# An LSTM step on TensorE: the first half's product for the second bank is cut into column pieces, and the last piece goes behind the second half's product for the first bank

## Chip, cores and metric

One Trainium2 chip, one of its cores. The metric is the time of one execution on the device in microseconds (us), as the median of several runs.

## The reference, cut to what matters

The kernel runs two graph layers, a state-space layer and at last an LSTM: `x` is (32, 512, 256), so the LSTM has a batch of 32, 512 time steps and 256 hidden units. Only the last layer is touched:

```python
def _lstm(x, W_ih, W_hh, b_ih, b_hh):
    x_proj = jnp.einsum('btd,gd->btg', x, W_ih) + b_ih + b_hh
    h0 = jnp.zeros((x.shape[0], W_hh.shape[1]), x.dtype)
    c0 = jnp.zeros_like(h0)
    def step(carry, xp):
        h, c = carry
        gates = xp + h @ W_hh.T
        i, f, g, o = jnp.split(gates, 4, axis=-1)
        c = jax.nn.sigmoid(f) * c + jax.nn.sigmoid(i) * jnp.tanh(g)
        h = jax.nn.sigmoid(o) * jnp.tanh(c)
        return ((h, c), h)
    _, hs = jax.lax.scan(step, (h0, c0), jnp.swapaxes(x_proj, 0, 1))
    return jnp.swapaxes(hs, 0, 1)
lstm_out = _lstm(x, W_ih, W_hh, b_ih, b_hh)
logits = jnp.einsum('bth,lh->btl', lstm_out, W_lin) + b_lin
g = argmax(logits, axis=-1)[..., None]
w = g * lstm_out
inc = jnp.cumsum(w, axis=1)
prefix, suffix = inc - w, inc[:, -1:, :] - inc
return 2.0 * lstm_out + prefix * fw_att + suffix * bw_att
```

The result is added to the layer's input `x`; the LSTM reads a layer-normalised `x`.

## The kernel before

The layers ahead of the LSTM run batch by batch and leave their result in a DRAM tensor `X3`, and the LSTM's weights, laid out anew, in `wr`. The function `recurrence` then goes through the 512 time steps, one after another, with the order of instructions on TensorE, VectorE and ScalarE written out by hand (`manual_schedule`). Each engine works through its own instructions in the order in which the code gives them.

**Layout of a step.** 256 hidden units are four quarters q of J = 64 units. The state of quarter q and the 32 batches lies on partitions 32q to 32q + 31, so gates and cell state fill all 128 partitions. Each quarter has two halves of H = 32 units. Of the gates of a quarter, 3H = 96 columns are g, f and i of the first half; the next 96 are g, f and i of the second half; then come 64 columns of o, for both halves, and two columns of which the first gives the difference of the two logits: W = 258 columns in all. They lie in two PSUM tiles, given by

```python
PARTS = ((0, 3 * H), (3 * H, W))
```

Bank 0 (`pg0`) has the 96 columns of the first half's g, f, i. Bank 1 (`pg1`) has 162 columns: g, f, i of the second half (0:96 within the bank), o of the first half (96:128), o of the second half (128:160) and the logit's two (160:162).

**Matmuls.** `h` is a list of two tiles, h0 and h1: the transposed state of the first and of the second halves, 128 x 32 each, the stationary operands. `part` (L1238) takes a list `order` of pairs (k, n): half k's product for bank n. For each pair it issues four matmuls, one for each quarter q, with 32 stationary columns each, into the 32 partitions of that quarter. In the trace each of these matmuls is two records of MATMUL and two of LDWEIGHTS. `x_part` (L1248) does the same for the input's part of the next time step. A step's state part has the order (0,0), (0,1), (1,0), (1,1) (L1295): both banks from h0, then both banks from h1.

**A step in order.**
- TensorE: the state part of this step (needs h0, and from (1,0) on h1), the input part of the next step, and in 4 of 16 steps two transposes of a coming input (L1181).
- ScalarE: tanh of bank 0 (L1302) into the tile `z`; tanh of 160 columns of bank 1 (L1303); tanh of the new cell state of each half (L1313, twice); a copy of one column (L1315).
- VectorE: for each half `ab` (L1308) and the new cell state in `z` (L1311). Then for each half `hh`, the new state (L1321), and its 32 x 32 transpose into `h` (L1325): first half 0, then half 1. After that `g` (L1332), one piece of other work out of the list `extra`, and `pp` (L1338), the running sum.

`extra` holds 16 pieces, one for each of 16 steps: 4 of `stats` (L1166 and L1167), 2 of `both` (two of L1172 each), and 10 of `results` for the 16 steps before (L1208 to L1220). In the first of the 16 steps a copy (L1340) comes on top.

The sigmoids are written with tanh, with factors of 0.5 in the weights, so all gates take one function.

Of the kernel before, what the change touches and what calls it, by code (L numbers as in the profile page):

```python
# [33 lines left out]
GB = 32  # L34
# [1085 lines left out]
def recurrence(ctx, tc, c, a, X3, wr, out):  # L1120
# [6 lines left out]
    H = J // 2  # L1127
    W = 4 * J + 2
# [13 lines left out]
    wih, whh = (wall[:, n * nw : (n + 1) * nw].rearrange("p (k q w) -> p k q w", k=DK, q=Q) for n in range(2))  # L1142
# [10 lines left out]
    def normalised(t0, out_):  # L1153


        mv = small.tile([P, NX, 2], F32, tag="mv", name=f"mv{t0}")
        rs = [None]
        xs = []
        for n in range(NX):
            xt = xp_.tile([P, D], F32, tag=f"xt{n}", bufs=1, name=f"xt{t0}_{n}")  # L1160
            nc.sync.dma_start(out=xt, in_=X3[t0 + 4 * n : t0 + 4 * n + 4].rearrange("t b d -> (t b) d"))
            xs.append(xt)

        def stats(n):
            bs = small.tile([P, 6], F32, tag="bs", name=f"bs{t0}_{n}")
            nc.vector.bn_stats(bs, xs[n])  # L1166
            nc.vector.bn_aggr(mv[:, n, :], bs)  # L1167
            if n == NX - 1:
                rs[0] = rstd_of(nc, small, c, mv[:, :, 1], NX, LN_EPS)

        def norm(n):
            nc.vector.tensor_scalar(  # L1172
                xs[n], xs[n], mv[:, n, 0:1], rs[0][:, n : n + 1], ALU.subtract, ALU.mult
            )
            nc.gpsimd.memset(xs[n][:, D - 1 :], 1.0)

        def turn(n):

            pt = psx.tile([P, DK, P], F32, tag="px", name=f"pxt{t0}_{n}")
            for k in range(DK):  # L1180
                nc.tensor.transpose(pt[:, k, :], xs[n][:, k * P : (k + 1) * P], c.ident)  # L1181
            g, r = n // 2, n % 2 * P
            if not r:
                out_[g] = xp_.tile([P, DK, 2 * P], F32, tag=f"xT{g}", name=f"xTr{t0}_{g}")
            xT = out_[g][:, :, r : r + P]
            return lambda: nc.scalar.copy(xT, pt)

        return tuple([lambda f=f, n=n: f(n) for n in range(NX)] for f in (stats, norm, turn))
# [48 lines left out]

    def part(pg, w, lhs, order, start, stop):  # L1238

        for k, n in order:  # L1240
            p, (s, e) = pg[n], PARTS[n]
            for q in range(Q):
                nc.tensor.matmul(  # L1243
                    p[q * GB : (q + 1) * GB, :], lhs[k], w[:, k, q, s:e],
                    start=(start and k == 0), stop=(stop and k == DK - 1),
                )

    def x_part(t, xT):  # L1248

        pg = [psg.tile([P, e - s], F32, tag=f"pg{n}", name=f"pg{n}_{t}") for n, (s, e) in enumerate(PARTS)]  # L1250
        r = (t % G) * GB
        part(pg, wih, [xT[t % CH // G][:, k, r : r + GB] for k in range(DK)], ((0, 0), (1, 0), (0, 1), (1, 1)), True, t == 0)
        return pg

    with tc.manual_schedule(engines={mybir.EngineType.PE, mybir.EngineType.DVE, mybir.EngineType.Activation}):
# [9 lines left out]
        pg = x_part(0, nxt)  # L1265
# [7 lines left out]
        h = hh = None  # L1273
        for t in range(T + 1):
            s = t % CH
            last = t == T
            if s == 0 and not last:
                t0 = t
                hh_was, pp_was = hh, pp
                hh = ch.tile([P, CH, J], F32, tag="hh", name=f"hh{t0}")  # L1280
                if t:
                    pp = ch.tile([P, CH + 1, J], F32, tag="pp", name=f"pp{t0}")
                assert not extra and not turning
                xT, nxt = nxt, [None] * 2
                stats, norms, turns = normalised(t0 + CH, nxt) if t0 + CH < T else ([], [], [])
                more = results(t0 - CH, hh_was, pp_was) if t else []
                both = [lambda fs=norms[n : n + 2]: [f() for f in fs] for n in range(0, len(norms), 2)]
                extra = stats + both + more
                turning = {(5, 6, 10, 11)[n]: f for n, f in enumerate(turns)}
            if last:  # L1290

                pg = [None, psg.tile([P, W - 3 * H], F32, tag="pg1", name="pglast")]
                part(pg, whh, h, ((0, 1), (1, 1)), True, True)
            elif t:
                part(pg, whh, h, ((0, 0), (0, 1), (1, 0), (1, 1)), False, True)  # L1295
            pgs = pg
            if not last:
                if t + 1 < T:
                    pg = x_part(t + 1, xT if t + 1 < t0 + CH else nxt)
                turned = [turning.pop(s)()] if s in turning else []  # L1300

                nc.scalar.activation(z[:, H : 4 * H], pgs[0], AF.Tanh)  # L1302
                nc.scalar.activation(z[:, 5 * H : 10 * H], pgs[1][:, : 5 * H], AF.Tanh)  # L1303
                z2 = st.tile([P, 12 * H + 1], F32, tag="z", name=f"z{t + 1}")
                for n in range(2):
                    c0 = 4 * n * H
                    ab = st.tile([P, 2 * H], F32, tag=f"ab{n}", name=f"ab{n}_{t}")
                    nc.vector.scalar_tensor_tensor(  # L1308
                        ab, z[:, c0 + 2 * H : c0 + 4 * H], 1.0, z[:, c0 : c0 + 2 * H], ALU.add, ALU.mult
                    )  # L1310
                    nc.vector.scalar_tensor_tensor(z2[:, c0 : c0 + H], ab[:, :H], 0.5, ab[:, H:], ALU.mult, ALU.add)  # L1311
                for n in range(2):
                    nc.scalar.activation(z[:, (10 + n) * H : (11 + n) * H], z2[:, 4 * n * H : (4 * n + 1) * H], AF.Tanh, scale=0.5)  # L1313

                nc.scalar.copy(z2[:, 12 * H :], level)  # L1315
                for f in turned:
                    f()
                h = []
                for n in range(2):
                    half = hh[:, s, n * H : (n + 1) * H]  # L1320
                    nc.vector.scalar_tensor_tensor(  # L1321
                        half, z[:, (8 + n) * H : (9 + n) * H], 1.0, z[:, (10 + n) * H : (11 + n) * H], ALU.add, ALU.mult
                    )
                    h.append(st.tile([P, GB], F32, tag=f"h{n}", name=f"h{n}_{t}"))
                    nc.vector.transpose(h[n], half)  # L1325
                z = z2
            if t:

                i = (t - 1) % CH
                p_, h_ = (pp_was, hh_was) if s == 0 and not last else (pp, hh)  # L1330
                g_ = st.tile([P, J], F32, tag="g", name=f"g{t}")
                nc.vector.scalar_tensor_tensor(  # L1332
                    g_, pgs[1][:, 5 * H : 5 * H + 1].to_broadcast([P, J]), level, h_[:, i, :], ALU.is_gt, ALU.mult,
                )
            if extra and not last:
                extra.pop(0)()
            if t:
                nc.vector.tensor_tensor(p_[:, i + 1, :], p_[:, i, :], g_, ALU.add)  # L1338
                if s == 0 and not last:
                    nc.vector.tensor_copy(pp[:, 0, :], p_[:, CH, :])  # L1340
# [5 lines left out]
        for n in range(4 * Q):  # L1346
            tq, q = n // Q, n % Q
# [20 lines left out]
@with_exitstack  # L1368
def kernel(ctx: ExitStack, tc: tile.TileContext, a, out):
    nc = tc.nc  # L1370
    nb = a.x.shape[0]
    const = ctx.enter_context(tc.tile_pool(name="const", bufs=1))
    dram = ctx.enter_context(tc.tile_pool(name="dram", bufs=1, space=DRAM))
    c = setup_consts(nc, const)
    X3 = dram.tile([N, nb, D], F32, name="X3")
    wr = dram.tile([P, 2 * DK * 4 * 258 + 2 * 64 + 1], F32, name="wr")
    odd = const.tile([1, 1], I32, name="odd")
    with ExitStack() as phase:
        layers_per_batch(phase, tc, c, a, X3, odd, wr)
    general = nc.values_load(odd, min_val=0, max_val=1, skip_runtime_bounds_check_because="it is only compared with 0")  # L1380
    with tc.If(general > 0):
        with ExitStack() as phase:
            layers_per_batch(phase, tc, c, a, X3)
    with ExitStack() as phase:
        recurrence(phase, tc, c, a, X3, wr, out)
# [70 lines left out]
```

## Time and profile before

| | us |
|---|---|
| median of 3 runs | 4697.27 (4695.42 to 4697.93) |
| profiled execution | 4702.24 |
| its span, first to last instruction | 4700.4 |

| engine | busy us over the span | share |
|---|---|---|
| PE (TensorE, matmul) | 3892.5 | 83% |
| PEld (TensorE, weight loads) | 2418.6 | 51% |
| DVE (VectorE) | 3388.8 | 72% |
| ACT (ScalarE) | 2926.4 | 62% |
| POOL (GpSimd) | 1332.6 | 28% |

| rows of the recurrence | records | mean ns |
|---|---|---|
| L1243 MATMUL, from h, 96 columns | 8176 | 252 |
| L1243 MATMUL, from h, 162 columns | 8176 | 301 |
| L1302 tanh of bank 0 | 512 | 251 |
| L1303 tanh of bank 1 | 512 | 305 |
| L1308 `ab` | 1024 | 221 |

A row of the profile's groups names the line of the kernel, the engine and the operation, what is written and read, the shapes and the count; behind the first bar stand the time in which at least one of them ran and the mean duration of one in ns, behind the second the idle time of the engine just before them, with what ended it. [...] The order in time shows runs of like instructions as one line: start in us from the span's start, length, engine, line.

### The profile page before, as it was taken

What the parts mean: (1) busy time and instruction counts of PE and PEld (TensorE: products, weight loads), DVE (VectorE), ACT (ScalarE), POOL (GpSimd) and SP (SyncE); (2) the same over time, 40 slices, a digit from 0 to 9 for tenths busy, and PEclk for the clock granted to TensorE, in tenths of its full rate; (3) what the DMA queues carried; (4) which work ended last, traced back from release to release, by engine and by line L of the source; (5) the groups of instructions that cost most, each with busy time, mean ns of one, the idle gap of its engine ahead of it and who ended that gap; (6) DMA issues with size and microseconds to landing.
All of it is one profiled execution on the core that took longest, in us unless ns stands there. A gap on an engine that the chain in (4) does not pass through costs nothing. (4 is left out here: it accounts for less than half of the span.)

```text
span 4700.4 us, 115757 instructions
## 1 busy us (share of the span) xinstructions
PE 3892.5 (83%) x46798; PEld 2418.6 (51%) x46798; DVE 3388.8 (72%) x10205; ACT 2926.4 (62%) x6724; POOL 1332.6 (28%) x1148
## 2 busy tenths in 40 slices
PE   3788888888888888888888888888688888888883
PEld 2344444444444544444444444444466666666662
DVE  3466676666666666666666676666489999999997
ACT  2577777777777777776677776766444444444442
POOL 3433333433333433333433333432100000000000
PEclk7899999999999999999999999999799999999997
DMA  4222111222111222111122211211212222222225
GB/s 114 60 64 71 59 59 57 64 73 71 59 59 57 64 73 71 59 59 57 58 70 70 64 62 57 63 51 50 63 35 44 44 44 46 46 47 44 44 42 164
DMA packets 273754, 288.69 MB, mean 61 GB/s; under 512 B 151872, under 2 KB 224536, under 8 KB 271032
## 3 DMA queue, kind: packets, MB, share of 16 engines
q1 hardware_dynamic: 269832, 271.32, 20.3%
q10 hardware_dynamic: 3216, 9.81, 0.7%
q8 instruction: 372, 6.09, 0.5%
q14 instruction: 174, 1.43, 0.1%
q0 software_dynamic: 160, 0.04, 0.0%
HBM read 227.09 MB, written 37.11 MB: 56 GB/s over the span
## 5 line engine op out<-in xcount | busy, mean ns | idle before, releaser
L1243 PE MATMUL pg<-wall,h 128*32 128x96 f32 x16352 | 559.2, 277 | 176.7 <-DVE h L1325 169.3
L1243 PEld LDWEIGHTS pg<-wall,h 128*32 128x32 f32 x16352 | 374.8, 109 | 350.3 <-DVE h L1325 331.8
L1243 PE MATMUL pg<-wall,xTr 128*32 128x96 f32 (+1 forms) x16384 | 549.0, 274 | 0.0
L467 DVE SCALAR_TENSOR_TENSOR w<-w,adjT 128x1024 f32<-128x1024 f32 x256 | 348.1, 1380 | 247.6 <-ACT w L461 247.6
L1243 PEld LDWEIGHTS pg<-wall,xTr 128*32 128x32 f32 x16384 | 447.7, 110 | 4.9 <-issue 0.3
L743 ACT ACTIVATE g<-bc,cs 128x128 f32<-128x128 f32 x1024 | 321.9, 391 | 137.3 <-PE py L811 137.3
L1302 ACT ACTIVATE z<-pg 128x96 f32<-128x96 f32 x512 | 128.7, 251 | 439.3 <-PE pg L1243 439.3
L693 DVE SCALAR_TENSOR_TENSOR acc<-px,convw,acc 128x511 f32<-128x511 f32 (+2 forms) x480 | 347.2, 745 | 75.8 <-ACT acc L688 68.0
L461 ACT ACTIVATE w<-rb,neg,colsa 128x512 f32<-128x512 f32 x512 | 387.4, 806 | 9.9 <-DMA rb<-linea 6.0
L729 POOL TENSOR_TENSOR ce<-ce,cT 128x384 f32<-128x384 f32 x128 | 185.2, 1477 | 667.7 <-ACT cT L701 650.5
L533 PE MATMUL pav<-w,hb 128*64 128x512 f32 x1024 | 352.5, 615 | 22.5 <-DVE w L467 22.5
L830 PE MATMUL po<-wc,xh 128*128 128x256 f32 x1024 | 283.4, 422 | 100.2 <-POOL xh L800 100.2
L1313 ACT ACTIVATE z<-z 128x32 f32<-128x32 f32 x1024 | 234.7, 229 | 168.0 <-DVE z L1311 100.8
L945 PE MATMUL pov<-wb,wv 128*128 128x257 f32 x1024 | 243.1, 390 | 89.3 <-DVE wv L467 89.3
L54 POOL TENSOR_SCALAR ve<-mv 128x4 f32<-128x4 f32 x32 | 6.2, 195 | 1064.1 <-DVE mv L1167 1064.1
L672 PE MATMUL px<-mT,win 128*128 128x512 f32 x640 | 305.2, 607 | 0.0
L830 PEld LDWEIGHTS po<-wc,xh 128*128 128x128 f32 x1024 | 203.2, 213 | 145.3 <-POOL xh L800 115.6
L945 PEld LDWEIGHTS pov<-wb,wv 128*128 128x128 f32 x1024 | 191.5, 192 | 133.1 <-DVE wv L467 105.3
L56 POOL TENSOR_TENSOR rs<-ve,mhalf 128x4 f32<-128x4 f32 (+1 forms) x192 | 255.2, 1329 | 15.9
L800 POOL TENSOR_TENSOR xh<-xh,zs 128x512 f32<-128x512 f32 x128 | 175.5, 1381 | 282.1 <-DVE xh L799 282.1
L1325 DVE STREAM_TRANSPOSE h<-hh 128x32 f32<-128x32 f32 x1024 | 216.7, 212 | 34.9
L672 PE MATMUL pz<-mT,win 128*128 128x512 f32 x512 | 240.4, 602 | 0.0
(243 smaller groups left out, 8492.0 us busy)
## 6 DMA issues: line engine op xcount, KB each, us to landing
bc<-line SPq DMA_DIRECT2D x128, 512.0 KB
adj<-in_adj_dram SPq DMA_DIRECT2D x32, 1024.0 KB
rb<-linea SPq DMA_DIRECT2D x64, 512.0 KB
ce<-line SPq DMA_DIRECT2D x64, 384.0 KB
x<-in_x_dram SPq DMA_DIRECT2D x32, 512.0 KB
X<-x SPq DMA_DIRECT2D x32, 512.0 KB
xt<-X SPq DMA_DIRECT2D x128, 128.0 KB
x<-X SPq DMA_DIRECT2D x128, 128.0 KB
```

The costliest lines, as they stand in the source:

```text
L56: nc.gpsimd.tensor_tensor(rs, ve, c.mhalf[:, :n], ALU.pow)
L461: nc.scalar.activation(w[:, t, k, :], rb[:, k, :], AF.Relu, bias=neg1, scale=cols[:, 2 * m + t, h + k : h + k + 1],)
L467: nc.vector.scalar_tensor_tensor(w[:, :, k, :], w[:, :, k, :], 1.0, edges, ALU.add, ALU.mult)
L533: nc.tensor.matmul(pa[k * HO : (k + 1) * HO, :], hb[:, j, 2 * q + k, :], w[:, t, k, :], start=(j == 0), stop=(j == NT - 1),)
L672: nc.tensor.matmul(pz, win[:, k, col : col + P], mT[:, k, :], start=(k == 0), stop=(k == DK - 1))
L693: nc.vector.scalar_tensor_tensor(acc[:, s:], pz[:, : N - s], convw[:, cc, k : k + 1], acc[:, s:], ALU.mult, ALU.add)
L743: nc.scalar.activation(g[:, i, k, :], bc[:, k, i * P : (i + 1) * P], AF.Relu, bias=cs[:, i, 2 * cc + k : 2 * cc + k + 1], scale=-1.0,)
L830: nc.tensor.matmul(po[:, i * D : (i + 1) * D], xh[:, cc, it * P : (it + 1) * P], wc[:, cc, :], start=(cc == 0), stop=(cc == NC - 1),)
L945: nc.tensor.matmul(po[:, : D + 1], ws[j // 2][:, j % 2, 0, it * P : (it + 1) * P], wb[:, j, :], start=(j == 0), stop=(j == NT - 1),)
L1243: nc.tensor.matmul(p[q * GB : (q + 1) * GB, :], lhs[k], w[:, k, q, s:e], start=(start and k == 0), stop=(stop and k == DK - 1),)
L1313: nc.scalar.activation(z[:, (10 + n) * H : (11 + n) * H], z2[:, 4 * n * H : (4 * n + 1) * H], AF.Tanh, scale=0.5)
L1325: nc.vector.transpose(h[n], half)
```

## The change

`part` takes entries with two more numbers, the first and the last column within the bank, and without them uses all columns as before. In the state part of every step from the second on, half 0's product for bank 1 comes in column pieces: 0:96 and 96:128 follow (0,0), then comes (1,0), and 128:162, the second half's o and the logit's columns, comes behind it, ahead of (1,1). Each piece is four matmuls, one for each q, with weight loads of their own. The input part and the last step give pairs.

```diff
     def part(pg, w, lhs, order, start, stop):
 
-        for k, n in order:
+
+        for k, n, *columns in order:
             p, (s, e) = pg[n], PARTS[n]
+            c0, c1 = columns or (0, e - s)
             for q in range(Q):
                 nc.tensor.matmul(
-                    p[q * GB : (q + 1) * GB, :], lhs[k], w[:, k, q, s:e],
+                    p[q * GB : (q + 1) * GB, c0:c1], lhs[k], w[:, k, q, s + c0 : s + c1],
                     start=(start and k == 0), stop=(stop and k == DK - 1),
                 )
...
             elif t:
-                part(pg, whh, h, ((0, 0), (0, 1), (1, 0), (1, 1)), False, True)
+                of_o = 3 * H, 4 * H, W - 3 * H
+                order = (0, 0), (0, 1, 0, of_o[0]), (0, 1, *of_o[:2]), (1, 0), (0, 1, *of_o[1:]), (1, 1)
+                part(pg, whh, h, order, False, True)
```

## The prediction

> **What bounds the kernel now.** I read the page for where the end is set, then the groups of the last stage with shapes kept apart, then one step of that stage in order of time, then the starts of single matmuls in the trace. All times below are from the profiled execution, 4702.24 us (span 4700.4, 1.84 us around it); the median of the runs is 4697.27, 5 us less. I take a saving per step from the profile and subtract it from the median.
>
> The change touches only the recurrence: 512 steps, from about 3410 us to 4640 us. The window 3850 to 4250 us lies inside it:
>
> ```profile
> core 0: us, PE busy (x) PEld busy (x) DVE busy (x) ACT busy (x) POOL busy (x), PEclk, DMA share, GB/s
> ...
> 3850.00:4250.00 400.00, 343.12 (x10716) 274.80 (x10708) 374.70 (x1897) 197.59 (x873) 18.81 (x60) 1.00 0.21 44
> ```
>
> DVE is busy 374.7 of 400 us, PE has its full clock (1.00). So VectorE is nearly full while the step is also a loop of dependences through TensorE and ScalarE. Which of the two ends last is read from the groups:
>
> ```profile
> L1243 PE MATMUL pg<-wall,h 128*32 128x162 f32 x7632 | 431.0, 301 | 0.0
> L1243 PE MATMUL pg<-wall,h 128*32 128x96 f32 x7632 | 345.6, 252 | 163.7 <-DVE h L1325 156.5
> L1308 DVE SCALAR_TENSOR_TENSOR ab<-z 128x64 f32<-128x64 f32 x955 | 210.8, 221 | 2.7
> L1303 ACT ACTIVATE z<-pg 128x160 f32<-128x160 f32 x477 | 145.4, 305 | 11.3
> L1302 ACT ACTIVATE z<-pg 128x96 f32<-128x96 f32 x477 | 119.9, 251 | 407.1 <-PE pg L1243 407.1
> ```
>
> The first tanh (L1302) waits for TensorE in every step; the second (L1303) sits idle only 11.3 us / 477 = 24 ns before it starts. L1308 hardly idles, although it needs L1302's result: VectorE's other work ends at almost the same moment. One step:
>
> ```profile
> 4002.16 0.21 DVE L1325 STREAM_TRANSPOSE h<-hh 128x32 f32<-128x32 f32 x1
> ...
> 4002.43 1.09 PE L1243 MATMUL pg<-wall,h 128*32 128x96 f32 x32 [0.43 <-DVE h L1325]
> 4002.53 0.21 DVE L1325 STREAM_TRANSPOSE h<-hh 128x32 f32<-128x32 f32 x1
> 4002.66 0.24 DVE L1332 SCALAR_TENSOR_TENSOR g<-pg,wall,hh 128x64 f32<-128x64 f32 x1
> 4002.82 0.68 DVE L1217 TENSOR_TENSOR m<-pp,wall 128x512 f32<-128x512 f32 x1
> ...
> 4003.31 0.25 ACT L1302 ACTIVATE z<-pg 128x96 f32<-128x96 f32 x1 [0.96 <-PE pg L1243]
> ...
> 4003.42 0.22 DVE L1338 TENSOR_TENSOR pp<-pp,g 128x64 f32<-128x64 f32 x1
> 4003.58 0.30 ACT L1303 ACTIVATE z<-pg 128x160 f32<-128x160 f32 x1
> 4003.59 0.23 DVE L1308 SCALAR_TENSOR_TENSOR ab<-z 128x64 f32<-128x64 f32 x1
> ```
>
> The loop is: h0 transposed, matmuls into bank 0, tanh, ab, z, tanh, hh, h0. The single records of the trace give its clock, counted in ns from the end of h0's transpose and the same within 2 ns in nearly all of the 490 steps I went through. One matmul of the program is two passes, and the four q run side by side on four column tiles, so the part of the state is eight groups of four records, at 55, 162 (0,0), 244, 382 (0,1), 519, 602 (1,0), 684, 822 (1,1). A 96-column pass thus takes 82.5, a 162-column pass 137.5: 0.833 ns a column plus 2.5. h1 is transposed at 362, its weight load goes out at 416, yet (1,0) starts at 519, just when (0,1) is through: TensorE is late by its own queue, not by h1. L1302 starts at 934, L1303 at 1209, ab of half 0 at 1217 (32 after L1302's end), ab of half 1 at 1587 (72 after L1303's end, so 40 to spare), the next h0 is there at 2401, the next h1 at 2763.
>
> How far could ab of half 0 move? Back to back, VectorE starts an instruction up to 82 ns before the end of the one ahead. In 10 steps of 16 (those after a 681 ns piece of `results`) ab overlaps it by 45: VectorE leaves 37 ns. In 3 (after a `stats`) VectorE was through 30 ns earlier: 112. In 2 (after `both`) it overlaps by 82 already, and in 1 (after `stats` and the copy of L1340) VectorE is 114 late: nothing to gain.
>
> **The change, part by part.** `part` takes slices of columns; the x part and the last step give pairs and issue what they did: 0. In the other 511 steps (0,1), eight records of 162 columns, becomes columns 0:96, 96:128 and 128:162, so three pieces, and the third stands behind (1,0). Columns streamed are the same. Added: 16 matmul and 16 weight-load records a step (64 + 64 become 80 + 80 with the x part). No wait is added: each bank still ends with the same kind of matmul, and the new pieces follow matmuls of their own engine. No DMA and nothing of SP or POOL moves. Behind on TensorE's queue stand the x part and, in 4 steps of 16, the transposes; before the next h0 the matmul row idles 430 ns (60 in those 4 steps), which hides some 10 ns later. That cover shrinks by what the loop gains, to about 10 in those 4 steps, so I take off half a microsecond (if it went wholly, 4 steps of 16 would lose some 10 ns each, 1.3 us).
>
> Unknown is a pass of four 32-column records, call it p. From the trace: the columns cost 27 ns, with the 2.5 added 29. Its four weight loads must fit under it: after h0's arrival the second loads of the four tiles start 28, 29, 28, 28 ns after the first ones, so a 32-column load takes some 28 and the four run side by side; matmul and load records of one pass go out within 27 ns. And where both are short, in L650/L651 (128-column load of about 107, 32-column stream of 27), weight loads follow each other by 108 to 112: the shorter hides under the longer, at 2 to 5 ns over it. So p is 29 to 33; I take 30, and 31.5 for 34 columns.
>
> [...] But here 96-column passes of four take 82.5, 20.6 a record, and records of different tiles start 1 to 14 ns apart[...]. [...] the trace's surcharge is 2.5. I take 30 [...]; below 29 nothing is left.
>
> The sum, again from h0: (0,0) at 55, 162; piece 0:96 at 244, 326; 96:128 at 409, 439; (1,0) at 469, 551 instead of 519, 602: 50 earlier. h1's load at 416 and 28 for it give 444, so h1 does not bind. 128:162 at 634, 665; (1,1) at 697, 834 instead of 684, 822: 12 later. L1302 starts at 884, L1303 at 1221, ends 1526; ab of half 1 not before 1558.
> - 10 steps: ab of half 0 gains 37 of the 50, then VectorE binds. ab of half 1 would be at 1550, but tanh gives 1558: 8 late, which goes to h1 and from it into the next step's VectorE work, about every other step. Gain 37 and 29 in turn: 33 each, 330.
> - 3 steps: about 48 each (h0's loop binds), 144.
> - 3 steps: 0. They are VectorE from h1 on.
> (330 + 144) / 16 = 29.6 ns; x 511 = 15.1 us; less 0.5 is about 14.5. 4697.3 - 14.5 = 4682.8.
>
> The same sum for other p: (1,0) moves by 109 - 2p, bank 1 by 4p - 108. At p = 33 the gain is some 12 us, at 35.5 9.4, at 40 4; at 42 it is gone, because L1303 is 60 late and its 40 of slack and the earlier h0 no longer pay for that.
>
> **The rivals.**
> - Short passes are dear, slower. Place: 128:162 between (1,0) and (1,1), which delays L1303 and so ab of half 1, z, h1. It decides from p = 42. At p = 52 L1302 is hardly earlier (109 - 104 = 5) and L1303 is 100 late, 60 beyond its slack: ab of half 1 at 1646, its z 252 after that, hh of half 0, next in VectorE's order, 108 later, h0 433 later, 2439 instead of 2401. That is 38 in most steps and less in the 3 where VectorE is last, 33 on the mean: x 511 = +17 us, 4714. [...] For: L1303 today waits for bank 1 (24 ns after L1302's end, while ScalarE starts a ready instruction up to 94 ns before the end of the one ahead), no 32-column pass of four is in this trace, and 32 more records must be issued. Against: the 28 ns loads and the 2.5 ns surcharge. Chance 0.20.
> - The gain at bank 0 is used up: p of 36 to 46, or VectorE and bank 1 take nearly all of it. For: DVE is at 94% and 3 steps of 16 gain nothing anyway. Then 4688 to 4706, middle 4694. Chance 0.16.
> - More than forecast: VectorE's work between h1 and ab closes up further than 82 ns of overlap, h0's loop alone binds: 49 x 511 = 25 us, 4672. Against: 82 is the deepest overlap of a pair there. Chance 0.05.
> - That the move does less than it says (only 34 of 162 columns, 57 ns, go behind (1,0), and the cut at 96, where nothing is moved, adds two passes' surcharge) is in the numbers already.
>
> **How the numbers follow.** Likeliest (0.59): 4682.8, own range 4680 to 4687 from p of 29 to 34. About 0.2%, 9.4 us, is what a measurement of this kernel can tell from no change. Faster by more: 0.59 + 0.05 = 0.64; within: 0.16; slower: 0.20. The range for 8 in 10 runs from 4678 (leaves out most of the third rival) to 4708 (takes in the second, leaves out most of the first).
>
> **What would show it.** Matmul records of L1243 from h: 24528 instead of 16352, a third each of them in new shapes of 96, 32 and 34 columns beside the old. Group starts 409, 439, 469; if 409 to 469 is over 84, the price of short passes was the error. L1302 884 after h0 instead of 934; the idle before L1303 up from 24 to about 85 ns; L1308 overlapping the instruction ahead by 82 in most steps; a step of about 2365 instead of 2401, with the `both` and copy steps unchanged. DVE's share of the window would rise above 374.7 of 400. A step longer than 2401 with L1308 of half 1 starting 32 after L1303's end is the first rival.

## The result and the profile after

| | us |
|---|---|
| before, median of 6 runs | 4698.57 (4695.42 to 4699.74) |
| after, median of 6 runs | 4715.47 (4710.46 to 4725.82) |
| ratio after / before | 1.0038, 95% interval 1.0026 to 1.0049 |
| profiled execution after | 4711.74 (span 4709.9) |

The change costs 17 us where 14.5 were to be won. The spread of the runs is no sign: the 6 runs of the changed kernel spread over 15 us and these 6 of before over 4, but 29 later runs of before, on another chip, spread over 15 too. The loss lies in the recurrence: in the profiled executions the time from the first h0 to the last is 1247.9 us, 1232.3 before, so 15.6 longer. (The spans differ by 9.5 only, because the stages ahead took 5 us less in this execution.) The forecast was wrong, and it is worth seeing how: almost every number of its sum can be found in the profile of the changed kernel, and yet the kernel is slower.

From the page, the span and the row of one DMA queue; then the row of the window 3850 to 4250 us:

```profile
span 4709.9 us, 132113 instructions
...
q8 instruction: 435, 7.13, 0.6%
```

```profile
3850.00:4250.00 400.00, 352.11 (x13136) 283.95 (x13138) 368.04 (x1867) 193.58 (x859) 19.33 (x60) 1.00 0.21 45
```

VectorE is less busy than before (368.0 of 400 us, from 374.7): on average a step became longer, not shorter. The groups of the recurrence (the lines of the file moved down by 2 to 4: L1243 is L1245, L1302 is L1306, L1303 is L1307, L1308 is L1312):

```profile
L1245 PEld LDWEIGHTS pg<-wall,xTr 128*32 128x32 f32 x15072 | 422.0, 109 | 37.9 <-issue 28.7 <-ACT z L1307 0.5
L1245 PEld LDWEIGHTS pg<-wall,h 128*32 128x32 f32 x22596 | 378.6, 110 | 264.0 <-DVE h L1329 249.2 <-issue 12.3 <-DVE hh L1325 0.8
L1245 PE MATMUL pg<-wall,h 128*32 128x96 f32 x11304 | 370.1, 250 | 120.1 <-DVE h L1329 113.3 <-issue 2.0
...
L1312 DVE SCALAR_TENSOR_TENSOR ab<-z 128x64 f32<-128x64 f32 x942 | 210.5, 223 | 19.8 <-ACT z L1306 9.9 <-ACT z L1307 8.2
...
L1307 ACT ACTIVATE z<-pg 128x160 f32<-128x160 f32 x471 | 143.6, 305 | 52.6 <-PE pg L1245 13.4
L1245 PE MATMUL pg<-wall,h 128*32 128x34 f32 x3768 | 125.6, 194 | 2.1 <-issue 1.6
L1245 PE MATMUL pg<-wall,h 128*32 128x32 f32 x3768 | 121.6, 194 | 0.3 <-issue 0.3
L1306 ACT ACTIVATE z<-pg 128x96 f32<-128x96 f32 x471 | 118.4, 251 | 379.6 <-PE pg L1245 379.6
```

Before, the weight loads read:

```profile
L1243 PEld LDWEIGHTS pg<-wall,xTr 128*32 128x32 f32 x15264 | 416.2, 109 | 3.7
L1243 PEld LDWEIGHTS pg<-wall,h 128*32 128x32 f32 x15264 | 349.3, 109 | 325.4 <-DVE h L1325 308.4
```

New in these rows is the word "issue" as the end of TensorE's idle time: 28.7 and 12.3 us before its weight loads. It stands for time in which the engine waited for nothing that the profile shows. L1312 now waits here and there (19.8 us, 2.7 before), 9.9 of it for L1306 and 8.2 for L1307. Most steps do not show this. The median distance from one L1306 to the next is 2379 ns (before: 2403), and the groups of four records in the state part start, in ns from the end of h0's transpose, at 55, 162, 245, 327, 410, 438, 470, 555, 638, 668, 698 and 842. (These distances, and not the durations, are what a pass of four costs: a 32-column record lasts 194 ns in the mean, and the next group starts 28 or 32 ns behind its own.) But the mean distance is 2441 (before: 2410). A few dozen steps are 0.2 to 1.1 us longer than the others. One of them, in order of time, cut to the tanh of bank 0, the first rows of TensorE behind its pause and those that wait for them:

```profile
3572.72 0.25 ACT L1306 ACTIVATE z<-pg 128x96 f32<-128x96 f32 x1 [0.89 <-PE pg L1245]
...
3573.68 0.11 PEld L1245 LDWEIGHTS pg<-wall,h 128*32 128x32 f32 x2 [1.02 <-issue]
3573.68 0.33 PE L1245 MATMUL pg<-wall,h 128*32 128x162 f32 x2 [0.70 <-issue]
...
3574.19 0.30 ACT L1307 ACTIVATE z<-pg 128x160 f32<-128x160 f32 x1 [1.21 <-PE pg L1245]
...
3574.52 0.23 DVE L1312 SCALAR_TENSOR_TENSOR ab<-z 128x64 f32<-128x64 f32 x1 [1.04 <-ACT z L1307]
```

TensorE stops for 1.02 us just short of the end of the state part: 45 of its 48 matmul records have gone, h1 has long been there, and the profile shows no semaphore that it waits for. Bank 1, L1307 and `ab` of half 1 come 1.04 us late with it.

I counted TensorE's records (MATMUL, LDWEIGHTS and the sequencer's) from the start of the program. Of 99 pauses from the recurrence on (over 170 ns from one record's start to the next, with no wait that explains it), 96 end at a record whose number is 78 more than a multiple of 256; the other 3 lie in the last step or behind it. And the DMA queue q8 in the page, `instruction`, brings packets of 16384 bytes, after 435 (7.13 MB), and before:

```profile
q8 instruction: 372, 6.09, 0.5%
```

63 packets more for 16356 more instructions is 260 each; with the distance of 256 between the pauses, I take a packet to be a block of 256 of TensorE's records. The totals agree: 372 and 435 such blocks hold 95232 and 111360, and TensorE has 94646 and 110998 records. In the kernel before, the ends of the blocks do not show: at 4 of 258 in the recurrence TensorE stands still for over 150 ns, and these are its ordinary waits for h0 (once) and ahead of the transposes of L1181 (three times, 229 ns). In the changed kernel it is 105 of 322. Counted against the median of the steps of the same kind (the same place among the 16), all steps together are 27 us too long, and 25 of these lie in steps with such a pause or right behind one.

### The profile page after: what moved, and what is told of

It reads as the page before. It is cut to its first block, busy times and chain, and to the rows that moved or that the text cites. A ratio compares the mean times of both kernels' runs of the same rounds, so it can differ in the third digit from the quotient of the medians.

```text
span 4709.9 us, 132113 instructions
## 1 busy us (share of the span) xinstructions
PE 3937.3 (84%) x54974; PEld 2463.9 (52%) x54974; DVE 3388.4 (72%) x10205; ACT 2924.2 (62%) x6724; POOL 1334.2 (28%) x1148
## 3 DMA queue, kind: packets, MB, share of 16 engines
q8 instruction: 435, 7.13, 0.6%
## 5 line engine op out<-in xcount | busy, mean ns | idle before, releaser
L1245 PE MATMUL pg<-wall,h 128*32 128x96 f32 x24528 | 582.9, 240 | 136.5 <-DVE h L1329 125.0
L1245 PE MATMUL pg<-wall,xTr 128*32 128x162 f32 (+1 forms) x16384 | 583.4, 274 | 13.8 <-issue 12.3
L1245 PEld LDWEIGHTS pg<-wall,h 128*32 128x32 f32 x24528 | 411.2, 110 | 288.3 <-DVE h L1329 272.6
L1245 PEld LDWEIGHTS pg<-wall,xTr 128*32 128x32 f32 x16384 | 459.2, 110 | 41.0 <-issue 30.7
L1306 ACT ACTIVATE z<-pg 128x96 f32<-128x96 f32 x512 | 128.8, 251 | 415.0 <-PE pg L1245 415.0
L56 POOL TENSOR_TENSOR rs<-ve,mhalf 128x4 f32<-128x4 f32 (+1 forms) x192 | 255.0, 1328 | 15.9
L1312 DVE SCALAR_TENSOR_TENSOR ab<-z 128x64 f32<-128x64 f32 x1024 | 228.8, 223 | 32.2 <-ACT z L1306 21.6
```

The lines of the kernel that those rows point to most:

```text
L56: nc.gpsimd.tensor_tensor(rs, ve, c.mhalf[:, :n], ALU.pow)
L1245: nc.tensor.matmul(p[q * GB : (q + 1) * GB, c0:c1], lhs[k], w[:, k, q, s + c0 : s + c1], start=(start and k == 0), stop=(stop and k == DK ...
L1312: nc.vector.scalar_tensor_tensor(ab, z[:, c0 + 2 * H : c0 + 4 * H], 1.0, z[:, c0 : c0 + 2 * H], ALU.add, ALU.mult)
```

## The experiments

Theory A, formed from this trace: TensorE's supply of instructions has become the bound. A step has 161 records instead of 129 (160 and 128 of matmuls and weight loads, and one of the sequencer), in less time, and a block of 256 is used up before the next one is there. Theory B, the rival: the number is innocent, and it is the place of the new pieces in the state part, the third one between (1,0) and (1,1) above all, that holds up bank 1. (B is the kind of the first rival in the prediction, which had foretold 4714.) Times are compared with runs of the kernel before on the same chip.

**e1_cut_not_moved.** The same three pieces, all ahead of (1,0): cut, but not moved.

```diff
-                order = (0, 0), (0, 1, 0, of_o[0]), (0, 1, *of_o[:2]), (1, 0), (0, 1, *of_o[1:]), (1, 1)
+                order = (0, 0), (0, 1, 0, 3 * H), (0, 1, 3 * H, 4 * H), (0, 1, 4 * H, W - 3 * H), (1, 0), (1, 1)
```

> Half 0's product for bank 1 is cut into the same three pieces, but all three stand ahead of (1,0), in the order of before. Same records per step as after (160 of TensorE), no move. Theory A (supply of instructions: TensorE's program comes in blocks of 16 KB, and 160 records in a step of 2.4 us use them up faster than the next block comes): the median step is about 2410 (9 ns later at L1302 and L1303 for two more surcharges), 4 us more, and stalls of 0.1 to 0.9 us at every so many records on top, some 15 to 35 us: 4715 to 4735. Theory B (the place: the third piece between (1,0) and (1,1) holds up bank 1 in some steps, the number of records is innocent): 4702, within 3 us.

Measured: 4712.33 us (4707.98 to 4721.35) against 4697.25, ratio 1.0029 (1.0017 to 1.0041). The step's median is 2421: 18 ns more, twice the forecast of 9, since the tanh of bank 0 (L1302 of before) comes at 952 and not 943. That is 9 us. The rest is pauses: 49 of 322 blocks late, the mean step 2444. The sum lies just below A's band and well above B's value, but over half of it is the longer step, so this run alone does not decide.

**e2_cut_in_x_part.** The state part of before; the pieces are put into the input part.

```diff
-        part(pg, wih, [...], ((0, 0), (1, 0), (0, 1), (1, 1)), True, t == 0)
+        part(pg, wih, [...], ((0, 0), (1, 0), (0, 1), *(((1, 1, 0, 3 * H), (1, 1, 3 * H, 4 * H), (1, 1, 4 * H, W - 3 * H)) if t else ((1, 1),))), True, t == 0)
...
+                order = (0, 0), (0, 1), (1, 0), (1, 1)
```

> State part as before; instead the input part's second product for bank 1 is cut into the three pieces 0:96, 96:128, 128:162, where TensorE has 400 ns to spare. Again 160 records a step. Theory A: stalls as in the changed kernel, those that fall into the input part hidden, the others not: 4710 to 4730, with the step's median unchanged at 2401. Theory B: nothing on the path is touched: 4698, within 3 us.

Measured: 4703.59 us against 4697.25, ratio 1.0015 (1.0008 to 1.0021). Slower, though nothing on the path of the step was touched: its median is 2404. It loses 6 us, below A's band and above B's. 30 of 322 blocks are late. At a step of 2.40 us and 161 records the supply nearly keeps up.

**e3_two_pieces.** The move with one cut less.

```diff
-                order = (0, 0), (0, 1, 0, of_o[0]), (0, 1, *of_o[:2]), (1, 0), (0, 1, *of_o[1:]), (1, 1)
+                order = (0, 0), (0, 1, 0, 4 * H), (1, 0), (0, 1, 4 * H, W - 3 * H), (1, 1)
```

> Two pieces, 0:128 ahead of (1,0) and 128:162 behind it: the same move with 144 records a step instead of 160. Theory A: a block of 256 lasts 1.78 steps, 4.2 us, more than the 3.8 us at which refills arrive in the changed kernel: the stalls are gone or few, and the forecast gain appears: L1302 about 880 after h0, a step of about 2370, 4683, up to 4690 if a few stalls stay. Theory B: the piece between (1,0) and (1,1) is still there: 4708 to 4716 like the changed kernel.

Measured: 4681.34 us (4679.17 to 4689.59) against 4697.25, ratio 0.9967 (0.9955 to 0.9979): 16 us faster. This is A's number. L1302's counterpart comes 879 after h0, the step's median is 2371, and 5 of 290 blocks are late. TensorE's waits in the recurrence (engine and line, what it waited for, us, times, longest):

```profile
PEld pg L1245 <- DVE h L1328: 292.5, 478, 1.0
...
PEld pg L1245 <- issue: 0.6, 1, 0.6
```

One pause is left in that list, 0.6 us (the other 4 late blocks end in the ordinary wait of the transposes, 0.23 us), where the changed kernel has these:

```profile
PEld pg L1245 <- issue: 41.1, 89, 1.1
...
PE pg L1245 <- issue: 17.7, 47, 0.8
```

**e4_after_half_x.** The changed kernel's state part with a shorter input part: from the second step on it leaves out the second half of the input's product, so the kernel computes something else, and only its time counts.

```diff
-        part(pg, wih, [...], ((0, 0), (1, 0), (0, 1), (1, 1)), True, t == 0)
+        part(pg, wih, [...], ((0, 0), (0, 1)) if t else ((0, 0), (1, 0), (0, 1), (1, 1)), True, t == 0)
```

> The changed kernel's state part as it is, with three pieces, but from the second step on the input part leaves out the second half of the input's product (half of its matmuls): 128 records a step as before. Theory A: no stalls, the gain of the order alone: 4680 to 4686, median step about 2370. Theory B: the state part is that of the changed kernel: 4708 to 4716.

Measured: 4684.59 us (4683.24 to 4693.53) against 4697.25, ratio 0.9973 (0.9961 to 0.9984). The three pieces in their place bring 12.7 us once a step has 129 records; the step's median is 2375, and its list of waits has no "issue" ahead of L1245. B falls here. Since the input part also has fewer columns to stream, e4 alone would leave open that it is this work, and not the records, that was missed; e3 and e8 keep all of it.

**e5_x_part_192 and e6_x_part_224.** More records, all in the input part. The state part is that of before in both. The diff shows the input part of e5; e6 cuts the second product for bank 1 in five pieces, at H, 2 * H, 3 * H and 4 * H.

```diff
-        part(pg, wih, [...], ((0, 0), (1, 0), (0, 1), (1, 1)), True, t == 0)
+        part(pg, wih, [...], ((0, 0), *(((1, 0, 0, H), (1, 0, H, 2 * H), (1, 0, 2 * H, 3 * H)) if t else ((1, 0),)), (0, 1), *(((1, 1, 0, 3 * H), (1, 1, 3 * H, 4 * H), (1, 1, 4 * H, W - 3 * H)) if t else ((1, 1),))), True, t == 0)
```

> The state part as before. In the input part, which has 400 ns to spare, the second product for bank 0 is cut into three pieces of 32 columns and that for bank 1 into three (0:96, 96:128, 128:162): 192 records a step. Theory A (supply): in the runs so far blocks of 256 records follow each other at 3.3 to 3.4 us where TensorE waits for them. 193 records a step then cannot go faster than 193 / 256 x 3.4 = 2.56 us, 0.15 us over the step of 2.41: about 75 us more, 4755 to 4785, with stalls at nearly every block. Theory B (the place of the pieces in the state part): 4698, within 3 us; eight passes of surcharge more, 20 ns, lie in the 400 ns.

> As the one before, with the input part's second product for bank 1 in five pieces of 32 (the last 34): 224 records a step. Theory A: 225 / 256 x 3.4 = 2.99 us a step, 0.58 us over 2.41: about 295 us more, 4970 to 5020, and the distance from block to block stays at 3.3 to 3.4 us. Theory B: 4698 to 4703. A third, that each short pass costs TensorE more than seen and fills the spare time: the rise from 192 to 224 would be even with that from 160 to 192, and the input part would end at the next h0.

Measured: e5 4924.56 us against 4700.26, ratio 1.0482 (1.0466 to 1.0498); e6, one run, 5138.42. B, which foretold no change, is out by some 224 and 438 us. The sizes that A gave were too small, 75 and 295: I had taken 3.3 to 3.4 us a block from the shortest distances after a pause. With supply as the bound throughout (364 of 386 and 445 of 449 blocks late) the median distance from block to block is 3.71 us in both, 14.5 ns a record. The mean step is 2.84 us with 193 records and 3.28 with 225: 14.7 and 14.6 ns a record. In e5's list of waits it is the longest of TensorE's:

```profile
PEld pg L1245 <- issue: 219.7, 283, 2.1
PE pg L1245 <- issue: 160.9, 225, 2.0
...
PEld pg L1245 <- DVE h L1328: 84.6, 215, 0.5
```

The third possibility, that short passes fill TensorE's spare time, would have shown as busy time; what grows is idle time with nobody to wait for.

**e7_two_pieces_96.** As e3, cut at 96.

```diff
-                order = (0, 0), (0, 1, 0, 4 * H), (1, 0), (0, 1, 4 * H, W - 3 * H), (1, 1)
+                order = (0, 0), (0, 1, 0, 3 * H), (1, 0), (0, 1, 3 * H, W - 3 * H), (1, 1)
```

> Two pieces as in the version that was faster, but cut at 96: 0:96 ahead of (1,0), 96:162 behind. 144 records a step. (1,0) could start at 409 after h0, h1's weight load holds it to about 445, so L1302 comes 20 ns earlier than with the cut at 128. Theory A with the prediction's sum: VectorE's 37 ns and L1303 (unchanged at about 1218) bind, so 4681, within 2 us of the cut at 128, at best 4678. If instead L1302 alone set the step, 10 us less: 4671.

Measured: 4703.14 us against 4700.26, ratio 1.0007 (0.9999 to 1.0015): the whole gain of e3 is gone, and I had expected none of it to go. There are two short pauses in the loop (0.33 and 0.17 us), so supply is not the reason. In most steps (1,0) starts at 438, not at 409, because it waits for h1, and after that wait its second pass starts 106 after the first, not 83 (behind the wait for h0 it is 107, from 55 to 162, before and after). These 24 ns and the 29 of the later start, 53 ns, stand in TensorE's queue ahead of bank 1. L1303's counterpart comes at 1267 (e3: 1218) and `ab` of half 1 starts 32 after its end, that is, it waits for it. The tanh of bank 0 is no earlier than in e3, either (877 and 879): h1 itself, late from the step ahead, comes at 383 (373 in e3, 362 before), and (1,0) waits for it.

**e8_two_pieces_and_x.** e3's state part, and 16 records more in the input part, where TensorE has time.

```diff
-        part(pg, wih, [...], ((0, 0), (1, 0), (0, 1), (1, 1)), True, t == 0)
+        part(pg, wih, [...], ((0, 0), (1, 0), (0, 1), *(((1, 1, 0, 4 * H), (1, 1, 4 * H, W - 3 * H)) if t else ((1, 1),))), True, t == 0)
```

> The faster version (two pieces, cut at 128), and in the input part the second product for bank 1 cut at 128 too: 160 records a step again, as in the changed kernel, 16 of them where TensorE has time to spare. Theory A (supply): with 192 and 224 records TensorE took a block of 256 every 3.71 us, 14.5 ns a record, so 161 records need 2.33 us of a step of 2.37 and every block that comes late stalls the step: 10 to 30 us of the 16 that the two pieces won are lost, 4692 to 4710. Theory B (only what lies in the state part counts): 4681, within 3 us.

Measured: 4697.82 us against 4696.84, ratio 1.0000 (0.9991 to 1.0008). The step's median stays that of e3 (2373), the mean goes from 2382 to 2419, 80 of 322 blocks are late: nearly all of the 16 us is lost to the number of records. Its waits:

```profile
PEld pg L1245 <- issue: 29.2, 70, 1.1
PE pg L1245 <- issue: 11.7, 28, 0.7
```

| kernel | records a step | median step, ns | mean step, ns | blocks late | us against before |
|---|---|---|---|---|---|
| before | 129 | 2403 | 2410 | 4 of 258 | 0 |
| e4 | 129 | 2375 | 2386 | 4 of 258 | -12.7 |
| e3 | 145 | 2371 | 2382 | 5 of 290 | -15.9 |
| e7 | 145 | 2405 | 2413 | 6 of 290 | +2.9 |
| e2 | 161 | 2404 | 2419 | 30 of 322 | +6.3 |
| e1 | 161 | 2421 | 2444 | 49 of 322 | +15.1 |
| e8 | 161 | 2373 | 2419 | 80 of 322 | +1.0 |
| after | 161 | 2379 | 2441 | 105 of 322 | +16.9 |
| e5 | 193 | 2790 | 2837 | 364 of 386 | +224.3 |
| e6 | 225 | 3326 | 3278 | 445 of 449 | +438.2 |

Records, steps and late blocks are of the profiled execution; a block is late when TensorE stands still for over 150 ns at its end, for whatever reason (all 4 of before and of e4, 4 of e3's 5, of e7's 6 and of the changed kernel's 105 are ordinary waits, for h0 or of the transposes); the last column is a difference of medians (e6: one run).

## Why the prediction was wrong, point by point

- *"Added: 16 matmul and 16 weight-load records a step ... No DMA and nothing of SP or POOL moves."* This is the step that failed. The records were given their time on the array and no price for being fetched (that "32 more records must be issued" stood among the reasons for the first rival, without a cost), and the page of before lists the queue whose packets keep step with them (q8, 372 packets for 94646 records). Estimated at the 14.5 ns a record of e5 and e6, 129 need 1.87 us of a step of 2.40, and 145 need 2.10; 161 need 2.33 of 2.38, and blocks do not come evenly (3.43 to 4.12 us apart from the 5th to the 95th hundredth in e6, where nearly every one is waited for). The cost: the step's mean is 62 ns over its median, 7 before; 55 x 511 = 28 us.
- *p is 29 to 33, 30 taken.* Right: 28 and 32 for the 32 columns, 30 and 30 for the 34. The first rival's p of 52 was my assumption, shown by no trace, and did not occur; that it foretold 4714 and 4715 came is chance.
- *A third of the records from h in each of the shapes of 96, 32 and 34 columns beside the old.* Not so: 32 and 34 columns have a sixth each (3768 of 22608 in the window), 96 have half, old and new together. Nothing in the sum rests on it.
- *(1,0) at 469, L1302 at 884, L1303 at 1221.* Measured 470, 888, 1228. The idle before L1303, foretold as about 85 ns, is 89.
- *10 steps gain 33, 3 gain 48, 3 gain 0.* By medians of each kind, the 10 gain 19 to 35 and the 3 gain 35 to 40. Two of the 3 "zero" steps lose 21 and 24: VectorE counts from h1 there, and h1 comes up to 22 ns later behind h0 (384, not 362), because `ab` of half 1 waits for L1303. Over 16 steps that makes 10 us, not 15. e4, with the same state part, measured 12.7. The mechanism held; the term was too large by a third. In e3, which gives bank 1 back 10 ns, it is 14 by the same count and 16 by the time.
- *DVE's share of the window would rise above 374.7.* It fell to 368.0, since the pauses lengthen the mean step. Read first, this row alone would have said that something outside the sum had come in.
- Sum: 10 us won by the order, 28 lost to pauses: +18 against +17 measured.

What stays open: why e1, with a longer step, has more late blocks than e2 with the same number of records, and what sets the 3.71 us. On the first: e1 has 96 of its 160 records in the state part, e2 64, but no run separates that, and the two profiles are also of e1's slowest execution and of one of e2's faster ones. In e5 the packet goes out some 1.2 us after TensorE has entered the block ahead, takes about 1.0, and 1.4 pass after it until TensorE enters the next block. The three add up to nearly 3.71; what ties them together is not shown. Other transfers made no difference to a packet's own time: in the changed kernel it was 1.1 us in the median, with under half a DMA engine busy beside it as well as with over eight.

The version to keep is e3: cut once, at 128 (16 us faster than before).

## What to carry to other kernels

Cutting a matmul into pieces cost instructions here as well as time on the array (16 records more a step in e8 than in e3: some 16 us): where an engine issues hundreds of short ones in a few us, count its records in a period of the loop, compare with what TensorE was given here where it waited throughout (one in 14.5 ns, e5 and e6), and make the move with the fewest pieces. When the median step improves and the mean gets worse, look at the outliers, and count instructions up to each pause: 96 of the 99 pauses stood a multiple of 256 records apart here, which pointed at the supply and not at any dependence. And a piece that stands ahead of a wait is also a cover; in e7, with too little left ahead of the wait for h1, (1,0) started at 438 instead of 409 and its second pass another 24 ns late, and bank 1 behind it came at 1267 instead of 1218 in L1303's start.

## What the runs showed of the hardware that was not expected

- The packets of queue q8 have 16384 bytes each, one for every 256 of TensorE's records (before: 372 for 94646; after: 435 for 110998). Where TensorE waited at nearly every block's end (e5, e6), a block of 256 came every 3.71 us in the median, 14.5 ns a record.
- A pause at a block's end lasted up to 2.8 us (e6); with 161 records in a step of 2.38 us (after) it came at one block end in three; with 145 in a step of 2.37 us (e3) at one in 290, with 129 (before) at none of 258.
- Four column tiles side by side took 28 to 32 ns for a float32 pass of 32 or 34 columns (after: 410, 438, 470 and 638, 668, 698). The second pass behind a wait started 106 or 107 ns after the first (e7: (1,0); before and after: 55 to 162), where passes of 96 columns otherwise follow each other by 82 to 85.
